# A graph kernel of four layers: how layer 0 turns its adjacency tiles and counts in-degrees

## The chip, the cores and the metric

The kernel runs on one core of a Trainium2 chip. A core has TensorE (PE: matrix products from SBUF into PSUM, with the stationary operand loaded by a separate instruction, PEld), VectorE (DVE), ScalarE (ACT), GpSimd (POOL), SyncE (SP, which here only issues DMAs) and 16 DMA engines. PSUM has eight banks that each hold 512 words of 4 bytes in each of 128 partitions. Every engine works through its own instructions in order; a DMA queue is filled by the engine that issues it.

The metric is the device time of one execution in microseconds (us), as the median of several. The change is judged against the kernel before on the same chip.

## The reference, cut to what matters

There are 2708 nodes with 512 features. `adj` is a symmetric 0/1 matrix of int32 with ones on its diagonal, but the kernel doesn't rely on the symmetry: layer 0 multiplies with the transposed matrix, layers 1 to 3 with the matrix itself.

```python
def _L0_gnn_ref(X, adj, weight):
    a = adj.astype(X.dtype)
    out = (a.T @ X) @ weight
    in_degree = a.sum(axis=0)
    norm = jnp.clip(in_degree, 1.0, None) ** (-0.5)
    return jax.nn.relu(out * norm[:, None])

def _L1_gnn_ref(X, A, W_nb, b_nb, W_line, b_line, neibor_num):   # 64
    Ab = A > 0
    keep = Ab & (jnp.cumsum(Ab.astype(jnp.int32), axis=1) <= neibor_num)
    cnt = keep.sum(axis=1, keepdims=True).astype(X.dtype)
    nb_mean = (keep.astype(X.dtype) @ X) / jnp.maximum(cnt, 1.0)
    xj = jax.nn.leaky_relu(nb_mean @ W_nb.T + b_nb)
    xi = jax.nn.leaky_relu(X @ W_line.T + b_line)
    return xi + jnp.where(cnt > 0, xj, 0)
...
# each layer: h = relu(layernorm(x)); x = x + layer(h, adj, ...)
```

Layer 2 is masked attention with eight heads, layer 3 a mean over neighbours. Layer 1 keeps the first 64 neighbours of a row, so it needs the column of the 64th one; layers 1 and 3 need the row's degree.

## The kernel before

**Tiling.** Nodes are cut into `NC` = 22 chunks of `R` = 126, the last one with 62. Layer 0 goes over `adj` once, in six groups of columns (`sizes` = 4, 4, 4, 4, 3, 3 chunks) and, within a group, over the 22 row chunks `m`. One step of this double loop is a unit; there are 132. For the chunks of a group, accumulators `acc` of one PSUM bank each stay open over the 22 units. The features enter as `h0[m]`, the product of the normalized x and the layer's weight, split by `halves` into two fp32r parts so that two fast products stand for one exact one. The last chunk has both parts in one tile, its second one in the rows from `TAIL` = 64, and needs one product.

**A unit's stages.** `staged` (L219) writes the loops out with a lag for each stage:

- lag 0, `load0` (L427): one DMA from SP brings 126 rows of `adj`, 506 columns wide, into `ai` (five buffers). In the first group the chunk of x is loaded, normalized, turned and multiplied by the weight beside it (`dense`, L229).
- lag 4, `count0` (L445): DVE casts `ai` to fp32r `ar` (L450), ACT squares it to bf16 `ab` (L452), DVE runs a cumulative sum along the columns into `cum` (L458) and stores its last column in `deg` (L466), from which the next group goes on.
- lag 5, `sign0` (L469): ACT's Sign of 63.5 - `cum`, with a sum over the columns, which tells where the 64th neighbour stands.
- lag 6, `multiply0` (L483): on PE eight products (four chunks, two halves; six in a group of three) with `ar` as the stationary operand (L348), then one product with `ab` for each chunk against an identity with ones beside it (`ident1`, L501). The latter turns the tile and sums its columns at once. DVE copies the sums out (L504), ACT copies the turned tile as int8 into `vT` (L513). With the last row chunk the column sums are added up (L508), the norm is made (L509 to L511), and after the products each accumulator is evacuated with relu and norm, by ACT and DVE in turn (L531, L535); POOL, or DVE in the last group, adds the old x (L537).
- lag 6, `save0` (L540): ACT's queue stores the x of the group before.

`vT` stays in SBUF, one tile for each group, and is read by layers 1 to 3: `vT[g][:, k, :]` has a column of `adj` in each partition and all rows along it.

**Buffers.** All PSUM tiles of this part share one ring of eight banks (`ps`, L123). `ar` and `ab` have three buffers each, `cum` two, x five (`XBUFS`); `hn` and `y` share a ring `t` of three.

**The hand-over to layer 1.** `stages1` is layer 1's `dense`: load x, normalize, turn, multiply by two weights (`product1`, L596). Its first three steps are put into the last group of layer 0 (`AHEAD`, at m = 9, 13 and 18); the others follow it. Beside them run `save_last` (lag 3), which stores the last group's x, and `spread_last` (lag 4), which spreads the columns of the 64th neighbours over all partitions (`lastr`). `rdeg` and `rcnt` are made from `deg` by DVE (L572 to L576). Then `aggregate` (L356) multiplies `h1` with `vT`, masked by `lastr` in `weight1` (L621).

**Order.** The program order of the loops is a priority. The scheduler of the language puts an instruction ahead of others on its engine when by its model it is ready earlier; on the chip each engine then keeps that order.

## Time and profile before

| What | us |
|---|---|
| median of three executions (lowest, highest) | 1851.69 (1848.1, 1854.51) |
| the profiled execution, its own time | 1852.72 |
| its span, first to last instruction | 1850.8 |
| first products of layer 0 (`acc`) start | 55.47 |
| last products of layer 0 (`acc<-tail`) start | 399.86 |
| layer 1's `nb_ps` and `line_ps` products, `acc`, on the chain of waits | from 413.58 |
| layer 1's aggregation, one piece of the chain | 570.63, for 188.72 |

The profile is one execution's record. A group of instructions has its line in the code, engine, operation, output and input tiles with their sizes, how many there were, busy us and the mean ns of one, then the idle time that the engine had just before them and what ended it. Durations of matmuls are modelled and overlap; the distance between starts tells PE's rate. Waits are put down to the semaphore that came last.

The same page shows how PE's products stand beside the loads of their stationary operand, and the share of DMA queues:

```profile
L348 PE MATMUL acc<-halves,ar 126*126 126x512 f32 x924 | 253.2, 413 | 6.5 <-ACT vT L513 3.5 <-DVE ar L450 2.6 <-DVE deg L466 0.3
L348 PEld LDWEIGHTS acc<-halves,ar 126*126 126x126 f32 x924 | 163.8, 187 | 51.0 <-issue 9.2
L473 ACT ACTIVATE cum<-cum,limit 126x504 int16<-126x504 int16 (+3 forms) x132 | 88.4, 670 | 62.1 <-DVE deg L466 60.0
...
q1 hardware_dynamic: 106812, 123.60, 23.1%
q10 hardware_dynamic: 18484, 33.28, 5.4%
```

q1 is the queue that SP fills, q10 that of ACT. Loads of `adj`, loads of x and the copies between layers are on q1.

### The profile page before, as it was taken

To read this page: it belongs to the slowest core of one execution; us is meant where nothing else is said; L and a number is where in the kernel's file an instruction comes from. 1 tells how busy PE (TensorE), PEld (TensorE's weight loads), DVE (VectorE), ACT (ScalarE), POOL (GpSimd) and SP (SyncE) were. 2 spreads that over 40 slices of the span, in tenths; PEclk is the share of its full clock that TensorE was granted. 3 is DMA by queue.
4 is the path that set the end of the run, shared out by engine and by line. 5 is a ranking of instruction groups with operands and counts; after the bars stand their busy time and mean duration, and the time that the engine had idled before them with its cause. 6 is when DMAs were issued, how large, how long until landed. Compare 5 with 4: busy or idle time off the path is not lost.

```text
span 1850.8 us, 30734 instructions
## 1 busy us (share of the span) xinstructions
PE 1805.7 (98%) x11878; PEld 1050.0 (57%) x11878; DVE 1323.8 (72%) x1997; ACT 843.7 (46%) x1536; POOL 211.8 (11%) x190
## 2 busy tenths in 40 slices
PE   9999999889999999999999999999999999999998
PEld 4556667654446887754444344444344455478786
DVE  4755888874444566687889999999999777533334
ACT  2545887762220000056697776776743566500000
POOL 0001011211110112156100000000000222100000
PEclk9999999999999999999999999999999999999999
DMA  7323555542223112253330220121112444303221
GB/s 243 117 79 106 150 161 149 144 127 65 68 73 82 45 45 67 65 159 102 96 91 18 60 56 15 56 61 40 29 32 51 119 137 133 103 23 105 96 67 44
DMA packets 126027, 161.03 MB, mean 87 GB/s; under 512 B 57394, under 2 KB 77982, under 8 KB 124990
## 3 DMA queue, kind: packets, MB, share of 16 engines
q1 hardware_dynamic: 106812, 123.60, 23.1%
q10 hardware_dynamic: 18484, 33.28, 5.4%
q0 software_dynamic: 576, 2.10, 0.3%
q8 instruction: 95, 1.56, 0.3%
q14 instruction: 60, 0.49, 0.1%
HBM read 111.34 MB, written 47.42 MB: 86 GB/s over the span
## 4 chain that ended last, share of the span: by engine, by line
PE 61%; DVE 16%; issue 5%; DMA 4%; ACT 2%; POOL 0%; SPq 0%; DVEq 0%; ACTq 0%; POOLq 0%
PE acc L348 25%; PE av L945 10%; DVE t L762 9%; PE nb_ps L186 8%; PE sums L945 4%; PE wh_ps L186 4%; PE self_ps L186 4%; PE line_ps L186 4%; DVE cum L458 4%; DMA rb<-rT 2%; PE hT_ps L214 1%; DMA ai<-in_adj 1%; DMA x<-x 1%; DVE ar L450 1%; ACT cum L473 1%
## 5 line engine op out<-in xcount | busy, mean ns | idle before, releaser
L762 DVE SCALAR_TENSOR_TENSOR t<-rb,ec,vT 126x2708 f32<-126x2708 f32 (+2 forms) x220 | 532.6, 2471 | 21.5 <-PE sums L945 12.4
L348 PE MATMUL acc<-halves,kt 126*126 126x512 f32 x1848 | 434.8, 395 | 3.7 <-DVE kt L623 2.1
L945 PE MATMUL av<-t,whs 126*32 126x451 f32 (+3 forms) x4576 | 436.6, 515 | 1.3 <-ACT whs L751 0.8
L348 PEld LDWEIGHTS acc<-halves,kt 126*126 126x126 f32 x1848 | 342.6, 186 | 92.5 <-DVE kt L623 6.2
L945 PEld LDWEIGHTS av<-t,whs 126*32 126x32 f32 (+1 forms) x4576 | 161.9, 110 | 205.5 <-issue 180.1
L348 PE MATMUL acc<-halves,ar 126*126 126x512 f32 x924 | 253.2, 413 | 6.5 <-ACT vT L513 3.5
L780 ACT ACTIVATE b<-t,eb 126x2708 bf16<-126x2708 f32 (+1 forms) x78 | 199.0, 2552 | 21.6 <-DVE t L762 21.4
L348 PEld LDWEIGHTS acc<-halves,ar 126*126 126x126 f32 x924 | 163.8, 187 | 51.0 <-issue 9.2
L623 DVE SCALAR_TENSOR_TENSOR kt<-lastr,index,vT 126x504 fp32r<-126x504 int16 (+3 forms) x154 | 110.4, 728 | 81.7 <-PE acc L348 81.5
L195 ACT ACTIVATE ln_rs<-ln_mv,eps 126x1 f32<-126x1 f32 x88 | 25.6, 294 | 283.9 <-DMA x<-x 199.2
L1170 DVE CAST kt<-vT 126x504 fp32r<-126x504 int8 (+3 forms) x154 | 56.0, 366 | 137.8 <-PE acc L348 137.8
L458 DVE TENSOR_TENSOR_SCAN cum<-ai,deg 126x504 int16<-126x504 int32 (+2 forms) x110 | 126.0, 1156 | 32.9 <-DMA ai<-in_adj 21.5
L945 PE MATMUL sums<-t,whs 126*32 126x338 f32 (+5 forms) x1568 | 141.0, 451 | 5.6 <-ACT out L984 5.6
L751 ACT ACTIVATE whs<-wh,ef 126x64 f32<-126x64 f32 x220 | 76.3, 349 | 128.3 <-PE sums L945 73.1
L912 POOL TENSOR_SCALAR z<-y 126x512 f32<-126x512 f32 x22 | 44.0, 2001 | 666.9 <-DVE y L905 658.2
L473 ACT ACTIVATE cum<-cum,limit 126x504 int16<-126x504 int16 (+3 forms) x132 | 88.4, 670 | 62.1 <-DVE deg L466 60.0
L945 PEld LDWEIGHTS sums<-t,whs 126*32 126x32 f32 (+1 forms) x1568 | 56.0, 109 | 73.3 <-issue 39.1
L191 DVE BATCH_NORM_STATS2 ln_st<-x 126x6 f32<-126x512 f32 x88 | 60.4, 686 | 48.7 <-DMA x<-x 40.9
L513 ACT CAST vT<-vT_ps 126x504 int8<-126x504 f32 (+1 forms) x132 | 70.1, 536 | 29.2 <-DVE sums L504 20.0
L186 PE MATMUL nb_ps<-wfn,hT 128*126 128x512 f32 x176 | 81.2, 605 | 2.0 <-ACT hT L216 2.0
L186 PE MATMUL nb_ps<-wn,hT 128*126 128x512 f32 x176 | 81.4, 606 | 0.0
L186 PE MATMUL h_ps<-w0s,hT 128*126 128x512 f32 x176 | 79.9, 597 | 1.4 <-ACT hT L216 1.1
(178 smaller groups left out, 1972.7 us busy)
## 6 DMA issues: line engine op xcount, KB each, us to landing
x<-x SPq DMA_DIRECT2D x105, 252.0 KB
x<-x ACTq DMA_DIRECT2D x84, 252.0 KB
ai<-in_adj SPq DMA_DIRECT2D x84, 249.0 KB
x<-in_x SPq DMA_DIRECT2D x42, 252.0 KB
rb<-rT SPq DMA_DIRECT2D x7, 1332.8 KB
wh<-whd SPq DMA_DIRECT2D x70, 94.5 KB
whd<-wh SPq DMA_DIRECT2D x21, 252.0 KB
aT<-avT SPq DMA_DIRECT2D x21, 252.0 KB
```

Source lines behind the costliest of these rows:

```text
L186: nc.tensor.matmul(po[:n], lhsT[:, f, :n], w[:, f, :], start=(f == 0), stop=(f == NF - 1))
L191: nc.vector.bn_stats(st[:n], xc[:n])
L348: nc.tensor.matmul(acc[:R], weight[:, k * R : (k + 1) * R], parts[:, i, :], start=(m == 0 and i == 0), stop=(m == NC - 1),)
L458: nc.vector.tensor_tensor_scan(cum[:n, :gw], ai[:n, :gw], ai[:n, :gw], 0.0 if g == 0 else deg[:n, m : m + 1], op0=ALU.add, op1=ALU.max,)
L473: nc.scalar.activation(cum[:n, :gw], cum[:n, :gw], AF.Sign, bias=limit[:n], scale=-1.0, accum_out=signs[:n, m, g : g + 1],)
L513: nc.scalar.copy(vT[g][:, :, m * R : (m + 1) * R], pt[:R, :K, :R])
L623: nc.vector.scalar_tensor_tensor(by_chunk(kt, cs), lastr[:, cs[0] * R : (cs[-1] + 1) * R].rearrange("p (c r) -> p c r", r=R), index[:R, m ...
L751: nc.scalar.activation(t[:q, :O], wh.pop((u, m))[:q], AF.Copy, scale=by)
L762: ins = nc.vector.scalar_tensor_tensor(t[:q, : hi - lo], row[h][:q, lo:hi], ec[:q, m, h : h + 1], vT[g][:q, k, lo:hi], op0=ALU.max, op1=AL ...
L780: nc.scalar.activation(b[:q, : hi - lo], weight[s][:q, : hi - lo], AF.Sigmoid, bias=eb[:q, m, h : h + 1], scale=STEEP,)
L945: nc.tensor.matmul(p[j * S : (j + 1) * S, : b - a], lhsT, rhs[:, part * size + a : part * size + b], start=(s % NC == 0), stop=(s % NC == ...
L1170: nc.vector.tensor_copy(by_chunk(kt, cs), pattern(m, cs))
```

## The change

Row chunks are taken in pairs. The 252 rows of chunks 2b and 2b+1 are dealt out so that the first holds the even rows and the second the odd ones (`paired`); the last 188 rows keep their natural order for the products. One DMA loads a pair: partition r of `ai` gets rows 2r and 2r+1 side by side. `ai` has three such double buffers in place of five single ones. For the last pair a second copy, in even and odd rows, is loaded beside the natural one (`both`).

- `ar` is now ACT's Square of `ai`, which also sums its row into `squares`. DVE's cast is gone, and so is `ab`; `squares` takes the place of `ind` in a later test of the input.
- DVE forms `two` = 256 x odd + even as int16, once a pair: two bytes that are the entries of two neighbouring rows. A DMA stores it in DRAM (`packed`), and a transposing DMA, one for each chunk of columns (`turn0`), reads 1360 rows x 128 columns of int16 back, so that partition = column and the bytes along it = rows in natural order. That is `vT`, now uint8 with 128 partitions. The turns of a group are issued in the next group at m = 4, 7, 10 and 13, those of the last group in layer 1's steps (`turn_last`, lag 4). PE's turns, DVE's copies of the sums and ACT's copies into `vT` are gone.
- The in-degrees come from products of ones (32 columns) with the upper 16 bits of `ar`, for both chunks of a pair in one block, chunk k into partitions 32k to 32k+31 of one bank (`sums_ps`) that stays open over the group. At m = 20 it is copied out, turned (`by_row`) and made into the norm, one unit before the group's end.
- Chunk 19's old x is loaded into the ring `t` in place of the ring of x.
- `deg` is in paired order: it goes through DRAM (`degd`) to come back in natural order as `rdeg`, from which `rcnt` is made. `spread_last` puts `lastr` into natural order and moves from lag 4 to lag 8.

```diff
+    oneb = const.tile([P, 32], BF16, name="oneb")
+    nc.gpsimd.memset(oneb, 1.0)
...
+    def paired(src, c):
+        if c >= NC - 2:
+            return natural(src, c)
+        first = c // 2 * 2 * R
+        return src[first : first + 2 * R, :].rearrange("(r e) d -> e r d", e=2)[c % 2]
...
             def load0(i):
...
-                ai = wk.tile([R, WG + P - R], I32, name="ai", bufs=5)
+                ai = wk.tile([R, 2, WG + P - R], I32, name="ai", bufs=3)
+                q = min(2 * R, N - m * R) // 2
+                block = adj[m * R : m * R + 2 * q, c0 : c0 + wide]
+                pairs = block.rearrange("(r e) w -> r e w", e=2)
+                if m < NC - 2:
+                    nc.sync.dma_start(ai[:, :, :wide], pairs)
+                    both = ai
+                else:
+                    both = wk.tile([R, 2, WG + P - R], I32, name="ai", bufs=3)
+                    nc.gpsimd.memset(both[:, :, :wide], 0)
+                    nc.sync.dma_start(both[:q, :, :wide], pairs)
+                    nc.gpsimd.memset(ai[:, 1, :gw], 0)
+                    nc.sync.dma_start(ai[:, 0, :gw], block[:R, :gw])
+                    move(nc.sync, ai[:last_rows, 1, :gw], block[R:, :gw])
+                    move(nc.sync, ai[TAIL : TAIL + last_rows, 1, :gw], block[R:, :gw])
...
             def count0(i):
...
-                nc.vector.tensor_copy(ar[:, :gw], ai[:, :gw])
-                nc.scalar.activation(ab[:n, :wide], ai[:n, :wide], AF.Square)
+                nc.scalar.activation(
+                    ar[:, :gw], ai[:, :gw], AF.Square, accum_out=squares[:R, m, g : g + 1]
+                )
...
+                if both is not None:
+                    two = wk.tile([R, WG + P - R], I16, name="two", bufs=1)
+                    nc.vector.scalar_tensor_tensor(
+                        two[:, :wide], both[:, 1, :wide], 256.0, both[:, 0, :wide],
+                        op0=ALU.mult, op1=ALU.add,
+                    )
...
             def sign0(i):
...
+                if two is not None:
+                    q = min(R, PAIRS - m // 2 * R)
+                    to = packed[g][m // 2 * R : m // 2 * R + q, :]
+                    nc.sync.dma_start(to, two[:q, : to.shape[1]])
+
+            def turn0(g, k):
+                nc.sync.dma_start(
+                    vT[g][:, k, : 2 * PAIRS].bitcast(I16),
+                    packed[g][:, k * R : k * R + P],
+                    transpose=True,
+                )
+                nc.gpsimd.memset(vT[g][:, k, N:], 1)
 
             def multiply0(i):
...
-                for k in range(K):
-                    nc.tensor.matmul(
-                        pt[:, k, :], ab[:n, k * R : k * R + P], ident1[:n], start=True, stop=True
-                    )
-                nc.vector.tensor_copy(sums[g][:, :K, m : m + 1], pt[:R, :K, R : R + 1])
...
-                nc.scalar.copy(vT[g][:, :, m * R : (m + 1) * R], pt[:R, :K, :R])
+                for j in (i, i + 1) if m % 2 == 0 else ():
+                    q = rows(m + j - i)
+                    for k in range(K):
+                        nc.tensor.matmul(
+                            sums[g][k * 32 : (k + 1) * 32],
+                            oneb[:q],
+                            tiles[j].bitcast(BF16)[:q, 2 * k * R + 1 : 2 * (k + 1) * R : 2],
+                            start=(j == i and m == 0),
+                            stop=(j > i and m == NC - 2),
+                        )
...
+                if g and m in (4, 7, 10, 13) and m // 3 - 1 < len(groups[g - 1]):
+                    turn0(g - 1, m // 3 - 1)
...
+        nc.sync.dma_start(
+            degd[:even].rearrange("(b f) r -> b (f r)", f=2).rearrange("b (r e) -> r b e", e=2),
+            deg[:R, :even].rearrange("r (b e) -> r b e", e=2),
+        )
+        nc.sync.dma_start(degd[even:].rearrange("c r -> r c"), deg[:R, even:])
         rdeg = const.tile([P, NC], F32, name="rdeg")
+        nc.gpsimd.memset(rdeg, 1.0)
+        nc.sync.dma_start(rdeg[:R], degd.rearrange("c r -> r c"))
```

## The prediction, made before the change was run

> **What bounds the kernel now.** First the page's busy times: TensorE (PE) is busy for nearly the whole span, and the change touches only layer 0 and its hand-over to layer 1.
>
> ```profile
> PE 1805.7 (98%) x11878; PEld 1050.0 (57%) x11878; DVE 1323.8 (72%) x1997; ACT 843.7 (46%) x1536; POOL 211.8 (11%) x190
> L458 DVE TENSOR_TENSOR_SCAN cum<-ai,deg 126x504 int16<-126x504 int32 (+2 forms) x110 | 126.0, 1156 | 32.9 <-DMA ai<-in_adj 21.5
> ```
>
> Second, busy time in the five groups after the first (their ends are the `acc<-tail` matmuls of the PE timeline: 173.72, 222.60, 272.55, 321.75, 363.01, 399.86 us). Columns: stretch, busy us of each engine, clock, DMA share, GB/s. PE leads, but DVE (85%) and ACT (81%) are close and DMA is half used.
>
> ```profile
> 174.00:222.00 48.00, 46.38 (x256) 34.04 (x255) 39.63 (x89) 37.07 (x85) 7.19 (x6) 1.00 0.52 151
> 222.00:272.00 50.00, 47.70 (x258) 34.31 (x259) 42.68 (x95) 40.37 (x93) 7.19 (x6) 1.00 0.53 155
> 272.00:321.00 49.00, 47.34 (x261) 34.26 (x259) 42.41 (x94) 40.33 (x93) 7.18 (x6) 1.00 0.52 153
> 321.00:363.00 42.00, 37.27 (x206) 26.12 (x204) 34.49 (x95) 31.91 (x88) 6.94 (x8) 1.00 0.51 147
> 363.00:400.00 37.00, 36.43 (x202) 26.07 (x201) 32.51 (x125) 31.17 (x95) 8.25 (x25) 1.00 0.40 117
> ```
>
> Third, the operations that the change takes away or moves, by shape, from 174 to 400 us:
>
> ```profile
> L501 PE MATMUL vT_ps<-ident,ab 126*128 126x128 bf16 x378 | 39.3, 222 | 2.3 <-ACT y L535 1.9 <-ACT vT L513 0.3
> L513 ACT CAST vT<-vT_ps 126x504 int8<-126x504 f32 x68 | 38.4, 571 | 12.7 <-DVE deg L466 8.6 <-DVE sums L504 3.8
> L450 DVE CAST ar<-ai 126x504 fp32r<-126x504 int32 x65 | 31.6, 487 | 5.2 <-PE acc L348 5.2
> L504 DVE COPY sums<-vT_ps 126x4 f32<-126x4 f32 x68 | 10.3, 157 | 0.0
> ```
>
> Fourth, PE's timeline inside a group (start, duration): eight products, four turns, again. A unit takes 282.58 - 280.43 = 2.15 us. Layer 1 runs the same products without turns (chain of waits: 188.72 us for 814, 0.232 us each), so eight cost 1.86 and the four turns 0.29 us, although their own starts spread over only 0.21.
>
> ```profile
> 280.43 2.10 PE L348 MATMUL acc<-halves,ar 126*126 126x512 f32 x8
> 282.37 0.40 PE L501 MATMUL vT_ps<-ident,ab 126*128 126x128 bf16 x4
> 282.58 2.10 PE L348 MATMUL acc<-halves,ar 126*126 126x512 f32 x8
> ```
>
> Fifth, where PE stands still: at group boundaries (here the third group begins), and where layer 1 begins. The brackets hold the idle time and what ended it.
>
> ```profile
> 226.08 0.73 PE L348 MATMUL acc<-halves,ar 126*126 126x512 f32 x2 [0.96 <-ACT vT L513]
> 227.07 1.42 PE L348 MATMUL acc<-halves,ar 126*126 126x512 f32 x5 [0.26 <-ACT vT L513]
> 229.09 0.38 PE L501 MATMUL vT_ps<-ident,ab 126*128 126x128 bf16 x4 [0.60 <-ACT y L535]
> ```
>
> ```profile
> 412.50 1.07 PE L214 MATMUL hT_ps<-ident,hn 126*128 126x126 f32 x4 [4.38 <-DVE hn L205]
> ```
>
> The brackets at the five boundaries add to 7.9 us (0.9, 2.8, 1.7, 1.4, 1.1); inside the groups PE waits three times for DVE `ar`, 2.6 us (1.94 of it at 343.37). By its units alone a group of four would take 20 x 2.15 + 3.37 = 46.4 us and one of three 20 x 1.63 + 2.6 = 35.2; the five are 16.5 us longer than that, of which the brackets name 10.5. So the turns and these stalls are on the path; the casts and copies of ACT and DVE matter only through the stalls.
>
> **What the skill says.** "TensorEngine Tiling (Array Packing)", Key Properties: 32-column tiles run in parallel, and changing the tiling mode drains the engine. Layer 2 agrees with the first: eight 32-column bf16 products of 338 columns start within 0.29 us (1340.24 to 1340.53). A change of width costs little: a one-column product starts 0.33 us after a 512-column one (usually 0.232), and the next wide one 0.1 after.
>
> ```profile
> 1340.24 0.51 PE L945 MATMUL sums<-b,parts 126*32 126x338 bf16 x8
> 1340.53 2.50 PE L945 MATMUL av<-t,whs 126*32 126x451 f32 x24
> ```
>
> "DMA: Bandwidth & Descriptors", the section on why a DMA increments its semaphore by 16: the number of engines is the largest k up to 16 that divides the outer dimensions. The trace agrees: while the last 46 output rows are stored (1846.65 to 1848.05), the queue uses 2 of 16 engines.
>
> ```profile
> q1 hardware_dynamic: 31, 0.06, 11.8%
> ```
>
> The same page, "Latency and other measured facts", gives 261 GB/s for transposing DMAs; no transposing DMA is in this trace.
>
> **The change, part by part.**
>
> PE, inside groups. A pair of units now pays 2 x 0.29 = 0.58 us for turns (four chunks), 2 x 0.24 = 0.47 (three chunks: 327.71 - 326.09 = 1.62 us a unit less six products). In its place comes one block of sums a pair: 8 or 6 products of 126 columns into 32-column strips. Bounds: 0.1 us if they pack as tightly as layer 2's, 0.9 us if each pays the turn's 0.07 and each switch 0.15. I take 0.24 for the products (the 36 ns spacing of layer 2, less for fewer columns, more for the two-byte stride), 0.18 for two switches, and 0.08 for the first wide weight load, which today also follows the turns: 0.50 and 0.45. That gains 0.08 x 44 pairs in the groups of four (11 of the 44 in the first group) and 0.02 x 22 in the groups of three: 4 us. So swapping PE work for PE work gives almost nothing.
>
> ACT loses `vT` (0.57 us a unit) and gains an accumulator read (0.19); `Square` stays and now writes `ar`. DVE loses `ar` and `sums` (2 x 0.64 = 1.29 us a pair) and gains `two`; the nearest row, L623, is 0.73 us for the same operation and width. Both engines get about 0.5 us a pair of slack. On the path this removes the stalls inside groups. One wait is new: `two` has a single buffer, so DVE's next `two` waits for the packed store of the pair before; behind it stand the scan, `deg` and the norm, for which ACT's signs and the evacuations wait. A store has a pair's time, 4.2 us, and loads of twice its size land in 2.7 to 2.8 us when nothing is ahead of them (chain, 203.43 and 207.91): taken at nothing, 1 us a pair (66 us) if that cover is gone for good, which only a DMA queue that is always full would do.
>
> Boundaries. Today the norm waits for the last unit's turns, their copies and a reduction, and new turns need banks that old accumulators hold. Afterwards the norm is ready a unit earlier. What is late next: the block of sums comes first in a group and needs a ninth bank, so it waits for the first accumulator's evacuation, 0.68 us of ACT, of which three last products (0.7) cover part. I take 1.0 us a boundary for banks and small stalls (bounds 0 and today's 3.3), and data apart (below).
>
> DMA. A group of four carries 7.5 MB today (153 GB/s x 49 us). Added: 11 packed stores of 127 KB, four transposes of 1360 x 256 B = 348 KB (an estimate of 1.3 us each from the skill's 261 GB/s) and a second copy of the last pair, 0.38 MB: 10.7 MB, share 0.52 to about 0.75. Mean rate suffices; bursts hurt. On SP the store, waiting for DVE, stands before the next pair's load; a transpose waits for all stores of its group, the last of them four units old; POOL's fill of its last columns waits for it in turn, and behind that only residual adds of the group's end. The second copy of the last pair has 94 rows, so k = 2: 188 runs of 2024 B at the 2-engine rate seen at the end (31 packets of 2 KB in 1.4 us, 45 ns each) take 8.5 us, and the next pair's load queues behind it on two engines. Three pair buffers give a load about four units, 8.6 us, before the squares need it. So it is about hidden; bounds 0 and 6 us a boundary, I take 0.9.
>
> Entry to layer 1. One residual moves to another ring, so the third x load no longer waits for a save (4.3 us) and its own 3.4 us. 4.4 us of stall go; the degrees' round trip through DRAM on SP, 2520 and 2772 single words, and the last group's three transposes stand before the next loads. Bounds: gain 4.4, loss 8. PE has two to three chunks of 6.9 us to hide it; I take a gain of 3. The spreads of `last`, four steps later, lie beside PE's products.
>
> Sum. A group of four: 10 pairs x (16 x 0.232 + 0.50) = 42.1, last pair 12 x 0.232 + 0.50 = 3.3, boundary 1.0: 46.4. A group of three: 10 x (12 x 0.232 + 0.45) + 2.5 + 1.0 = 35.8. Three and two: 210.8, and 0.5 for layer 1's early turns: 211.3, where today 173.72 to 399.86 is 226.1: -14.8, 3 from the swap and 12 from stalls. First group -0.9, entry -3, two-engine loads 5 x 0.9 = +4.5. Together -14. The profiled execution took 1852.7 us (span 1850.8), 1.0 above the median of three: 1838.7, say 1839.
>
> **Rivals.**
> - Forecast, 1830 to 1846: 0.42.
> - PE reaches its product rate: sums pack to 0.1 us and no boundary stalls: -0.4 x 66 pairs, -4.5, -5: about 1812 to 1830. For it: layer 1's 188.72 us without a stall. Against: a switch costs something. 0.12.
> - No change, 1846 to 1857: the block of sums costs 0.7 us, which is +13 and cancels the boundaries. For it: the drain; against: the 0.1 us seen around narrow products. 0.15.
> - Slower: the last pair's second copy. If SP issues it before the pair's own rows, or the next pair comes two units late, squares and PE wait 6 us at each of five boundaries: +30 - 14, about 1868. It decides once landing takes more than the four units of lead. For it: k = 2, and DMA waits of 2.5 to 4.4 us already in the chain. Against: PE has rarely waited for data. With packed stores late behind loads (one buffer for `two`) adding to it: 0.31.
>
> Under 0.3% (5.5 us) a measurement of this kernel can't be told from no change. Faster 0.54, same 0.15, slower 0.31. The likeliest case's own range is 1830 to 1846; with the others, 1818 to 1868.
>
> **What would show it.** The five groups take about 46 and 36 us; the block of sums takes about 0.5 us between products; no stall ends with DVE `ar`; the stall before layer 1's third turn is gone. Wrong if PE waits for ACT squares or DMA at each group's start, if DVE stands before `two`, or if transposes take over 5 us.

## The result and the profile after

| | before | after |
|---|---|---|
| median of four executions (lowest, highest), us | 1851.71 (1848.1, 1854.51) | 1921.05 (1916.96, 1928.38) |
| span of the profiled execution, us | 1850.8 | 1915.0 |
| first products of layer 0 start, us | 55.5 | 54.5 |
| first group, us | 118.2 | 123.2 |
| the five other groups, us | 48.9, 50.0, 49.2, 41.3, 36.9; together 226.1 | 61.2, 62.3, 64.5, 49.7, 54.1; together 291.8 |
| end of layer 0 to layer 1's aggregation, us | 170.5 | 168.9 |
| from there to the end, us | 1280.4 | 1276.5 |

The ratio after to before is 1.038, 95% interval 1.0343 to 1.0416: slower by 69 us where 13 us of gain were forecast. The parts of the table add up to the 64.2 us between the spans: -1.0 + 5.0 + 65.7 - 1.6 - 3.9. The five groups hold the loss. (A group is counted from one start of `acc<-tail` to the next; the sums are rounded once, the expectations below have 226.2 and 291.9.)

The page's busy times, and the two groups of instructions that stand for the waits, of the changed kernel:

```profile
PE 1823.6 (95%) x11884; PEld 1064.8 (56%) x11884; DVE 1304.2 (68%) x1792; ACT 803.4 (42%) x1542; POOL 217.7 (11%) x203
...
L494 DVE TENSOR_TENSOR_SCAN cum<-ai,deg 126x504 int16<-126x504 int32 (+2 forms) x110 | 128.4, 1178 | 49.9 <-DMA ai<-in_adj 44.0
L522 ACT ACTIVATE cum<-cum,limit 126x504 int16<-126x504 int16 (+3 forms) x132 | 88.2, 668 | 119.7 <-DVE deg L502 113.5
```

ACT and DVE did get lighter (ACT 843.7 to 803.4, DVE 1323.8 to 1304.2 us), as the change means them to. But DVE's scan now stands 44 us before loads of `adj` where it stood 21.5, and ACT's Sign waits 113.5 us for that scan where it waited 60.0. PE's share fell from 98% to 95% although its busy time rose by 18 us. The busy times by group say how both can be (columns as before: stretch, busy us of PE, PEld, DVE, ACT, POOL, granted clock, DMA share, GB/s):

```profile
178.00:239.00 61.00, 49.64 (x262) 35.39 (x261) 36.91 (x55) 30.74 (x87) 8.75 (x6) 0.92 0.55 159
239.00:301.00 62.00, 52.07 (x261) 37.05 (x260) 36.21 (x58) 32.34 (x93) 8.00 (x10) 0.86 0.64 165
301.00:366.00 65.00, 51.47 (x263) 36.95 (x264) 39.80 (x60) 33.49 (x97) 8.54 (x10) 0.89 0.66 165
366.00:415.00 49.00, 38.92 (x194) 26.66 (x192) 29.78 (x58) 25.52 (x85) 8.18 (x10) 0.92 0.63 163
415.00:470.00 55.00, 42.88 (x205) 28.99 (x205) 33.51 (x90) 28.03 (x98) 7.81 (x19) 0.87 0.57 137
sum 292.00, PE 234.99 PEld 165.04 DVE 176.21 ACT 150.12 POOL 41.28; mean PE 47.00 PEld 33.01 DVE 35.24 ACT 30.02 POOL 8.26
```

The same stretch of the kernel before in one row:

```profile
174.00:400.00 226.00, 215.12 (x1176) 154.79 (x1176) 191.72 (x493) 180.84 (x450) 36.75 (x51) 1.00 0.50 146
```

PE's idle time went from 226 - 215 = 11 us to 292 - 235 = 57 us: 46 us of the loss are PE standing still. The other 20 us are PE's work at a lower clock, 0.86 to 0.92 where it was 1.00. That it is the clock, and not the new block of sums, is seen in a run told of below, no_pack: with the same products at a clock of 0.99, PE is busy 213.9 us over its five groups (columns as above).

```profile
198.25:439.01 240.76, 213.87 (x1183) 152.54 (x1181) 141.78 (x266) 146.93 (x454) 29.90 (x25) 0.99 0.47 139
```

No engine and no mean DMA share is near its end (DMA 0.55 to 0.66); the loss is waiting, not work.

PE's timeline in the second group shows the good part and the bad part side by side (start, duration):

```profile
242.53 3.71 PE L369 MATMUL acc<-halves,ar 126*126 126x512 f32 x14
246.17 0.30 PE L558 MATMUL sums_ps<-ar,oneb 126*32 126x126 bf16 x8
246.40 3.98 PE L369 MATMUL acc<-halves,ar 126*126 126x512 f32 x16
250.31 0.30 PE L558 MATMUL sums_ps<-ar,oneb 126*32 126x126 bf16 x8
...
258.80 0.24 PE L558 MATMUL sums_ps<-ar,oneb 126*32 126x126 bf16 x4
264.10 0.30 PE L558 MATMUL sums_ps<-ar,oneb 126*32 126x126 bf16 x4 [5.06 <-ACT ar L488]
264.32 5.91 PE L369 MATMUL acc<-halves,ar 126*126 126x512 f32 x13
```

Where data are there, the block of eight sums costs 246.40 - 246.17 = 0.23 us, and a pair takes 250.31 - 246.17 = 4.14 us where two units before took 4.30. Then PE stands 5.06 us before the odd chunk's `ar`, and the products after that stall take 5.91 / 13 = 0.45 us each where 3.98 / 16 = 0.25 is usual. "TensorE: Matmul & The Clock Gate", section on HAM oscillation (HAM is its name for what sets TensorE's clock by how busy it is), says that idle gaps of over some 3.4 us let the clock be throttled; this stall agrees, and it makes each long stall cost more than its own length.

What the waits of the changed kernel between 178 and 470 us are (engine, line, what it waited for: us, times, longest):

```profile
ACT cum L522 <- DVE deg L502: 80.4, 54, 8.2
...
PE sums_ps L558 <- ACT ar L488: 52.4, 27, 5.1
DVE two L506 <- DMA packed<-two: 50.0, 15, 10.1
DVE cum L494 <- DMA ai<-in_adj: 35.2, 20, 7.4
ACT ar L488 <- DMA ai<-in_adj: 20.1, 10, 6.1
```

The profile puts the third of these lines down to the single buffer of `two`; the fourth and fifth are the loads. They hold DVE; DVE's scan holds ACT's Sign; behind that Sign stands the next square, and for the square PE waits.

The chain of waits around the start of the second group (start, us, what) has the longest of the loads:

```profile
214.67 1.27 DVE cum L494
215.94 0.58 DVE two L506
...
216.97 11.53 DMA ai<-in_adj
...
228.58 0.70 DVE two L506
229.29 5.25 DMA ai<-in_adj
...
234.63 2.43 DVE cum L494 x2
```

The 11.53 us are the second copy of the last pair, 94 rows; `two` can't be formed before it, DVE holds everything behind `two`, and the next pair's load ends 5.25 us after it. The timelines of SyncE's queue, of DVE and of ACT (start, duration) show how little lead the copy had and who stood behind it:

```profile
216.97 0.69 SPq L475 DMA_DIRECT2D ai<-in_adj  x1
...
217.79 0.15 DVE L502 CAST deg<-cum 126x1 f32<-126x1 int16 x1
228.58 0.69 DVE L506 SCALAR_TENSOR_TENSOR two<-ai 126x506 int16<-126x506 int32 x1 [10.64 <-DMA ai<-in_adj]
...
230.78 0.71 ACT L522 ACTIVATE cum<-cum,limit 126x504 int16<-126x504 int16 x1 [8.17 <-DVE deg L502]
231.49 0.61 ACT L488 ACTIVATE ar<-ai 126x504 fp32r<-126x504 int32 x1
```

The copy was issued at 216.97, behind a store for which the queue had waited for DVE; at 217.94 DVE had nothing left to do before it, and stood 10.64 us. While the copy's rest arrived alone, from 224.2 to 228.4 us, SyncE's queue used 13.1% of the 16 DMA engines, which is two:

```profile
q1 hardware_dynamic: 104, 0.21, 13.1%
```

The same happens where the next two groups end. The copies are issued at 280.36 and 344.53, and DVE forms their `two` 11.5 us later each time. Here the profile names another transfer, the store of the `two` before, which landed about then; that DVE waited for the copy as well is seen in the run two_t below:

```profile
291.83 0.69 DVE L506 SCALAR_TENSOR_TENSOR two<-ai 126x506 int16<-126x506 int32 x1 [10.14 <-DMA packed<-two]
356.08 0.69 DVE L506 SCALAR_TENSOR_TENSOR two<-ai 126x506 int16<-126x506 int32 x1 [10.07 <-DMA packed<-two]
```

The hand-over to layer 1, on PE's timeline:

```profile
478.74 0.59 PE L215 MATMUL hT_ps<-ident,hn 126*128 126x126 f32 x4
...
489.08 1.07 PE L215 MATMUL hT_ps<-ident,hn 126*128 126x126 f32 x4 [2.88 <-DVE ln_mv L194]
```

The third chunk's turn, at 478.74, has no bracket any more (4.38 us before), but a chunk later PE stands 2.88 us.

### The profile page after: what moved, and what is told of

It is laid out like the page before. It is cut to its first block, busy times and chain, and to the rows that moved or that the text cites. A ratio compares the mean times of both kernels' runs of the same rounds, so it can differ in the third digit from the quotient of the medians.

```text
span 1915.0 us, 30559 instructions
## 1 busy us (share of the span) xinstructions
PE 1823.6 (95%) x11884; PEld 1064.8 (56%) x11884; DVE 1304.2 (68%) x1792; ACT 803.4 (42%) x1542; POOL 217.7 (11%) x203
## 4 chain that ended last, share of the span: by engine, by line
PE 67%; DVE 13%; DMA 12%; issue 6%; ACT 2%; POOL 0%; SPq 0%; DVEq 0%; ACTq 0%; POOLq 0%
PE acc L369 25%; PE av L1038 12%; PE nb_ps L187 8%; DVE t L855 7%; DMA ai<-in_adj 6%; PE sums L1038 5%; PE wh_ps L187 4%; PE self_ps L187 4%; PE line_ps L187 4%; DVE cum L494 3%; DMA packed<-two 3%; PE hT_ps L215 2%; PE h_ps L187 1%; PE fused_ps L312 1%; DMA rb<-rT 1%
## 5 line engine op out<-in xcount | busy, mean ns | idle before, releaser
L855 DVE SCALAR_TENSOR_TENSOR t<-rb,ec,vT 126x2708 f32<-126x2708 f32 (+2 forms) x220 | 532.2, 2469 | 17.2 <-PE sums L1038 9.4
L1038 PEld LDWEIGHTS av<-t,whs 126*32 126x32 f32 (+1 forms) x4576 | 166.4, 110 | 199.3 <-issue 173.4
L369 PE MATMUL acc<-halves,ar 126*126 126x512 f32 x924 | 259.2, 431 | 1.0 <-ACT y L611 1.0
L369 PEld LDWEIGHTS acc<-halves,ar 126*126 126x126 f32 x924 | 179.5, 201 | 52.8 <-issue 6.1
L1263 DVE CAST kt<-vT 126x504 fp32r<-126x504 uint8 (+3 forms) x154 | 56.0, 365 | 138.2 <-PE acc L369 138.2
L522 ACT ACTIVATE cum<-cum,limit 126x504 int16<-126x504 int16 (+3 forms) x132 | 88.2, 668 | 119.7 <-DVE deg L502 113.5
L488 ACT ACTIVATE ar<-ai 126x504 fp32r<-126x504 int32 (+2 forms) x132 | 75.4, 572 | 61.8 <-DMA ai<-in_adj 25.7
L506 DVE SCALAR_TENSOR_TENSOR two<-ai 126x506 int16<-126x506 int32 (+2 forms) x66 | 44.3, 672 | 72.5 <-DMA packed<-two 53.6
## 6 DMA issues: line engine op xcount, KB each, us to landing
x<-x SPq DMA_DIRECT2D x105, 252.0 KB
x<-x ACTq DMA_DIRECT2D x84, 252.0 KB
x<-in_x SPq DMA_DIRECT2D x42, 252.0 KB
whd<-wh SPq DMA_DIRECT2D x21, 252.0 KB
aT<-avT SPq DMA_DIRECT2D x21, 252.0 KB
```

Source lines behind the costliest of these rows:

```text
L369: nc.tensor.matmul(acc[:R], weight[:, k * R : (k + 1) * R], parts[:, i, :], start=(m == 0 and i == 0), stop=(m == NC - 1),)
L488: nc.scalar.activation(ar[:, :gw], ai[:, :gw], AF.Square, accum_out=squares[:R, m, g : g + 1])
L522: nc.scalar.activation(cum[:n, :gw], cum[:n, :gw], AF.Sign, bias=limit[:n], scale=-1.0, accum_out=signs[:n, m, g : g + 1],)
L855: ins = nc.vector.scalar_tensor_tensor(t[:q, : hi - lo], row[h][:q, lo:hi], ec[:q, m, h : h + 1], vT[g][:q, k, lo:hi], op0=ALU.max, op1=AL ...
L1038: nc.tensor.matmul(p[j * S : (j + 1) * S, : b - a], lhsT, rhs[:, part * size + a : part * size + b], start=(s % NC == 0), stop=(s % NC == ...
L1263: nc.vector.tensor_copy(by_chunk(kt, cs), pattern(m, cs))
```

## The experiments

Eighteen kernels were run. Each was compared with the kernel before on the same chip. Where an edit leaves work out, the groups' lengths are what is read: the later layers then work on other bits.

| kernel | median, us | ratio to before (95%) | first group | five groups |
|---|---|---|---|---|
| before | 1851.7 | 1 | 118.2 | 226.1 |
| after | 1921.05 | 1.038 (1.0343 to 1.0416) | 123.2 | 291.8 |
| two_t | 1918.56 | 1.0374 (1.0338 to 1.0409) | 123.8 | 282.4 |
| store7 | 1920.01 | 1.0368 (1.0338 to 1.0399) | 124.1 | 286.7 |
| split | 1899.58 | 1.0271 (1.0225 to 1.0317) | 117.3 | 274.6 |
| one_copy | 1885.93 | 1.0185 (1.0155 to 1.0216) | 120.7 | 257.5 |
| no_turn | 1937.67 | 1.0477 (1.0447 to 1.0508) | 120.8 | 282.2 |
| no_store_both | 1892.34 | 1.0232 (1.0202 to 1.0262) | 114.5 | 244.6 |
| no_pack | 1886.78 | 1.0197 (1.0167 to 1.0226) | 114.1 | 240.8 |
| no_store_sign6 | 1890.16 | 1.0215 (1.0185 to 1.0244) | 112.7 | 250.7 |
| ar_dve | not read | | 126.5 | 271.7 |
| two_loads | 1879.61 | 1.0146 (1.0111 to 1.0182) | 114.1 | 260.1 |
| sign6 | 1877.61 | 1.0136 (1.0106 to 1.0165) | 119.3 | 245.4 |
| loads_sign6 | 1866.81 | 1.0077 (1.0048 to 1.0107) | 112.8 | 244.5 |
| loads_sign6_one | 1865.96 | 1.0079 (1.006 to 1.0098) | 112.7 | 252.0 |
| loads_store7 | 1863.17 | 1.0051 (1.0033 to 1.0068) | 112.7 | 244.9 |
| six | 1891.69 | 1.0225 (1.0201 to 1.0249) | 130.7 | 254.5 |
| six_one | 1901.61 | 1.0277 (1.0249 to 1.0305) | 131.8 | 267.0 |
| t2_before | 1856.79 | 1.0026 (1.0009 to 1.0043) | 117.5 | 233.4 |
| pair_t2_before | 1866.08 | 1.0083 (1.0054 to 1.0112) | 121.5 | 236.9 |

The lengths come from one profiled execution of each kernel; how far they vary from one execution to the next was not measured. Two kernels whose queues wait alike (two_t and store7) lie 4 us apart in the five groups, so a difference of 5 us or less is not leant on.

### The single buffer of `two`

two_t:

```diff
-two = wk.tile([R, WG + P - R], I16, name="two", bufs=1)
+two = common.tile([R, WG + P - R], I16, name="two", tag="t", bufs=3)
```

> The changed kernel with `two` moved from its single buffer into the ring `t` (three buffers, shared with hn and y). Theory A (DVE waits at `two` for the packed store of the pair before, and everything behind it on DVE is late): most of the 65 us go, about 1870 to 1885 us, and the waits of DVE `two` on the packed store, 53.6 us now, fall under 10. Theory B (the last pair's second copy on two DMA engines holds up the next group): less than 10 us, about 1912 to 1920. Theory C (stores and transposing DMAs make the queue late for the pair loads, of which only three are buffered): less than 15 us, since the loads stay as late; DVE then waits for `ai` instead.

Measured: 1918.56 us, no gain. The five groups, 282.4, are 9.5 us shorter in the profiled execution, but layer 0 began 5.4 us later in it. The waits of two_t between 184 and 467 us show why so little came:

```profile
DVE two L506 <- DMA ai<-in_adj: 58.9, 15, 11.4
PE sums_ps L558 <- ACT ar L488: 45.7, 28, 5.1
```

`two` no longer waits 50 us for its store but 58.9 us for a load (10.6 us in the changed kernel, in one wait). Four of these waits, 39.5 us together, are for the second copy; in the groups where the changed kernel's profile had named the store they are

```profile
297.16 0.69 DVE L506 SCALAR_TENSOR_TENSOR two<-ai 126x506 int16<-126x506 int32 x1 [10.97 <-DMA ai<-in_adj]
359.63 0.69 DVE L506 SCALAR_TENSOR_TENSOR two<-ai 126x506 int16<-126x506 int32 x1 [11.38 <-DMA ai<-in_adj]
```

So a large part of what the profile put down to the single buffer was the copy, and the buffer alone was worth nothing that can be measured in the whole time.

### The second copy of the last pair

split gives the 94 rows to two transfers, of 80 and of 14 rows:

```diff
-nc.sync.dma_start(both[:q, :, :wide], pairs)
+cut = q // 16 * 16
+nc.sync.dma_start(both[:cut, :, :wide], pairs[:cut])
+nc.sync.dma_start(both[cut:q, :, :wide], pairs[cut:])
```

> The changed kernel with the second copy of the last pair loaded as 80 + 14 rows in place of 94. Theory B: the load of 11.5 us falls to about 4, the groups' ends lose their wait and some 6 us in each of six groups go: about 1880 to 1890 us. Theory A: about 5 us or less, 1912 to 1920. Theory C: about 10 us.

one_copy takes it out altogether:

```diff
-both = wk.tile([R, 2, WG + P - R], I32, name="ai", bufs=3)
-nc.gpsimd.memset(both[:, :, :wide], 0)
-nc.sync.dma_start(both[:q, :, :wide], pairs)
...
+both = ai
...
```

> The changed kernel without the second copy of each group's last pair: the packed numbers of the last two chunks are formed from the rows as the products use them, so the last rows of vT are not the ones that layers 1 to 4 should see (every step after layer 0 does the same work on other bits). Everything else is as changed. If the second copy costs what `split` gave back and a little more (its pair buffer and its bytes go too): five groups 262 to 270 us in place of 291.9, total 1888 to 1898. If the second copy's cost is only the queue that it sits on: about as `split`, 272 to 276, total 1900. If the loop of three pair buffers is the whole loss: below 240, total 1868.

Measured: the five groups fall by 17.2 us with split and by 34.3 with one_copy; the medians by 21 and 35 us. So the copy with its pair buffer is half of what the groups lost, and half of that again is gained by sending its rows as 80 and 14. In split the copy at the first of these boundaries has landed 3.77 us after its second part is issued (chain of waits), and DVE stands 3.60 us for it where it stood 10.64; at the next two boundaries that `two` comes after both scans, and DVE does not stand before it:

```profile
212.81 3.77 DMA ai<-in_adj
...
216.71 0.69 DVE L508 SCALAR_TENSOR_TENSOR two<-ai 126x506 int16<-126x506 int32 x1 [3.60 <-DMA ai<-in_adj]
```

one_copy did better than its first expectation and well short of the last one: the copy is the largest single cause, not the only one.

### The transposes, the stores and the packing

no_turn leaves out the transposing DMAs, no_store_both also the stores and the second copy, no_pack also `two`:

```diff
-nc.sync.dma_start(vT[g][:, k, : 2 * PAIRS].bitcast(I16), packed[g][:, k * R : k * R + P], transpose=True)
-nc.gpsimd.memset(vT[g][:, k, N:], 1)
+nc.gpsimd.memset(vT[g][:, k], 1)
```

> The changed kernel without its transposing DMAs: vT is filled with ones, so layers 1 to 3 work on another pattern and only layer 0's time is to be read. Theory C: 20 us or more go in layer 0. Theories A and B: under 8 us. The range of single transposes: 22 times the estimate of 1.3 us is 29 us of queue time in all.

> The changed kernel without the packed stores, the transposing DMAs, `two` of the last pair and the second copy (vT filled with ones; only layer 0's time is to be read). What is left is the pair loads with three buffers, the squares on ACT and the sums from ones. If A, B and C are all there is, groups of four take 45 to 47 us and groups of three 35 to 37 as predicted, some 1835 to 1845 us in all; if they stay above 55, the pair loads themselves (theory D) are the cause.

> `no_store_both` without the packing on VectorE as well: no `two`, no stores, no transposes, no second copy (vT is filled with ones by GpSimd; every later step does the same work on other bits). What is left of the change in layer 0 is pair loads, the casts of ar by squares on ScalarE, and the sums by ones. If the packing holds the loop (VectorE's 0.7 us for a pair between two scans, which needs both halves): five groups 228 to 233 in place of 244.6. If the squares on ScalarE behind the Signs hold it: 240 to 245.

In all three the fills of `vT` were put at the start of the program, and layer 0 begins near 84 us in place of 54.5; their medians can't be compared, their groups can. Measured, five groups: 291.8 after, 282.2 without transposes (61.2, 62.3, 64.5 against 63.3, 61.4, 61.0 in the groups of four; the last group gains 7), 244.6 without stores and copy too, 240.8 without packing too. Read beside one_copy's 257.5, stores and transposes together cost 13 us once the copy is gone, the packing 4, which is within the spread. Even with nothing of the new path left but pair loads, squares and sums by ones, the groups take 14.6 us longer than before. PE is busy for 213.9 us of them (shown above), 215 before; it stands 26.9 us where it stood 11, and most of it for ACT's square, where the kernel before waited 2.6 us for DVE's cast:

```profile
PE sums_ps L540 <- ACT ar L486: 20.6, 26, 2.4
```

no_pack's waits of SyncE's queue (185 to 430 us) tell what the loads then stand before:

```profile
SPq L470 <- ACT ar L486: 90.3, 29, 5.4
SPq L470 <- ACT cum L510: 32.7, 11, 7.2
```

L470 is the load of a pair. Its buffer is free when the square of the odd chunk has read it, so a late square makes a late load, which makes a late scan and a late Sign, and the next square is behind that Sign. This ring is read from the waits; no run opens it cleanly.

### ScalarE's order, half loads, and the casts

sign6 (with split and two_t) issues the Sign one unit later, behind the next chunk's square, and gives `cum` a third buffer; two_loads (with split) brings each pair as two transfers; loads_sign6 has all of these; ar_dve (with split) gives the cast back to VectorE:

```diff
-cum = wk.tile([R, WG], I16, name="cum", bufs=2)
+cum = wk.tile([R, WG], I16, name="cum", bufs=3)
...
-(5, sign0),
+(5, store0),
+(6, sign0),
```

```diff
-nc.sync.dma_start(ai[:, :, :wide], pairs)
+for e in range(2):
+    nc.sync.dma_start(ai[:, e, :wide], pairs[:, e])
```

```diff
-nc.scalar.activation(ar[:, :gw], ai[:, :gw], AF.Square, accum_out=squares[:R, m, g : g + 1])
+nc.vector.tensor_copy(ar[:, :gw], ai[:, :gw])
```

> The split kept, `two` in the ring `t`, `cum` with three buffers in the space so won, and the Signs one unit later (lag 6; the stores stay at lag 5). Theory E: a square no longer waits behind the Sign of the unit before it, PE's waits on ACT `ar` (46.7 us with the split) fall to 15 or less: 1860 to 1875 us. Theory D: under 10 us, 1890 to 1900.

> The 80 + 14 split kept (1899.6 us), and each pair loaded by two DMAs, even rows first, into the same buffer. Theory D (pair loads: a buffer is filled and freed in pieces of 0.5 MB, so the loop load, scan, Sign, Square, next load is too long for three buffers): the first half lands some 2 us earlier, that is once a loop of two pairs, and the groups fall by 5 to 10 us each: 1860 to 1880 us. Theory E (the squares that PE needs stand on ACT behind Signs that wait for DVE's scan): under 10 us.

> The split kept, and `ar` cast by DVE as in the kernel before, ahead of the scan; ACT keeps the Signs alone, and the test that all entries are 0 or 1, which used the squares' sums, is left out. Theory E: PE's waits on `ar` fall and some 20 us go, although DVE gets 0.4 us a unit more: 1870 to 1885 us. Theory D: no gain, 1890 to 1905. If DVE becomes the bound, the units take 2.2 us and more and the time goes up.

> Both: the later Signs with three `cum`, `two` in the ring `t`, the split, and each pair in two loads. If D and E both hold, the gains add and the groups come to 48 and 38 us: about 1850 us. If one alone holds, this equals the better of the two single ones within 6 us. If neither, about 1895 us, and the queue's load (theory C) is what is left.

Measured, against split's 274.6 us in the five groups: sign6 245.4, two_loads 260.1, both 244.5, the cast on DVE 271.7. ar_dve makes the kernel take its general path after layer 0 (5989 us), so its whole time says nothing. Moving the cast gains nothing that can be told from the spread: DVE's busy time rises to 209 us of 272, and PE still waits 28 us for DVE's `ar` (47 for ACT's in split). sign6's edits and a load that is there by halves do help, but not one on top of the other: both together give no more in these groups than sign6 alone; in the first group half loads save 6.5 us (119.3 to 112.8). How much of sign6's 29 us is the order of ScalarE is not shown, since `two` in the ring of three and the third `cum` came with it and split with these two alone was not run.

no_store_sign6 tried the later Sign where stores, transposes and copy are left out:

> `no_store_both` (no stores, no transposes, no second copy; vT filled with ones) with `two` still made, in the ring of three, and the test of the row sums one unit later, behind the next chunk's square. If ScalarE's order holds the loop: five groups 228 to 234 in place of 244.6. If it is the packing: 241 to 246.

Measured 250.7 us, no better than no_store_both's 244.6: a miss. The same edits that help while stores and the copy are there don't help without them, so ScalarE's order is not shown to be a cause by itself. It is worth a look that sign6, with all of its stores, transposes and the split copy, has groups as short (245.4) as no_store_both, which has none: what remains against 226.1 is not the added traffic alone.

### What is left in the best variant

loads_sign6_one is loads_sign6 without the second copy; six gives it six buffers of one chunk for three of a pair; six_one is both.

```diff
-ai = wk.tile([R, 2, WG + P - R], I32, name="ai", bufs=3)
+ai = [wk.tile([R, WG + P - R], I32, name="ai", bufs=6) for e in range(2)]
```

> `loads_sign6` (`two` in the ring of three, the test of the row sums one unit later, half loads) without the second copy of the last pair, left out as in `one_copy`, and with the pair buffers as in the change. If the second copy's buffer and bytes at the boundary are what is left (five groups 244.5 against 226.2): 228 to 234, total 1850 to 1856, within 0.3% of the kernel before. If half loads, and the wait of each pair for its buffer, are what is left: 240 or more, total 1862 to 1867.

> `loads_sign6` with the three buffers of a pair made into six of one chunk, so that the even chunk's buffer can be filled again as soon as its own square, its own scan and the packing have read it. Nothing is left out. If what is left of the loss (five groups 244.5 against 226.2) is that a pair is held as one: 234 to 238, total 1857 to 1861. If the loads wait for bandwidth or for the queue rather than for a buffer: 242 to 246, total 1865 to 1869. If more and shorter loads delay the stores: over 248, over 1870.

> `six` without the second copy of the last pair (left out as in `one_copy`). If the boundary of a group is the rest of the loss, since two buffers and 0.38 MB go to the second copy there: five groups 226 to 232, total 1848 to 1854, level with the kernel before. If the turned stores and the order on ScalarE are the rest: 236 or more, over 1857.

loads_sign6_one: 1865.96 us against 1866.81, nothing; its groups were even 7.5 us longer, and the hand-over to layer 1 as much shorter. In one_copy leaving out the copy was worth 34 us in the groups; with the other repairs in place it is hidden. The costs overlap, and their sizes can't be added.

six and six_one got slower, by 25 and 36 us against loads_sign6 and loads_sign6_one. 18 and 19 us of that lie in the first group, beside the loads of x. With more buffers the scheduler set ScalarE's instructions in another order: in six, from 74 to 84 us, a Sign that waits 4.04 us for DVE stands ahead of the turned x (`hT`), for which PE then waits 1.39 us. That this order is the whole loss is not shown. So these two don't answer what they were built for; whether a buffer for each chunk helps stays untried in a clean form.

store7 and loads_store7 issue the store of `two` two units later. In the changed kernel SyncE's queue stood for VectorE at the stores (L533) between 178 and 470 us, with the next loads behind:

```profile
SPq L533 <- DVE deg L502: 42.2, 21, 3.9
SPq L533 <- DVE two L506: 30.7, 16, 3.5
```

```diff
+(7, store0),
```

> `two_t` (`two` in the ring of three) with the store of `two` issued two units later than the scan of its row, so that it does not stand at the head of SyncE's queue while VectorE still works on `two`; nothing else is changed and nothing is left out. In the changed kernel SyncE waited 57 us (178 to 400 us of the span) for VectorE at these stores, with the next loads behind them. If that is a cause of its own: five groups 255 to 265 in place of 282.4, total 1890 to 1901. If the loads are held by their buffers and only trade one wait for another: 278 to 285, total 1914 to 1921.

> `loads_sign6` with the store of `two` two units later in the same way; nothing is left out. If what is left (five groups 244.5 against 226.2) is the store at the head of the queue: 228 to 234, total 1850 to 1856. If it is the buffers of the pairs, which ScalarE's squares set free: 242 to 247, total 1864 to 1869.

Measured: 1920.01 us against two_t's 1918.56, and 1863.17 against loads_sign6's 1866.81 (intervals of the ratios overlap); five groups 286.7 and 244.9. store7 hardly did what it was built for. Against two_t, on which it is built, the queue's wait for VectorE at the stores went from 63 us only to 60 (184 to 467 and 180 to 467 us), and the loads' own wait at the queue, for buffers mostly, stayed near 80. loads_store7 did take some away, 51 us to 36 (168 to 412 us), and its groups are as long as those of loads_sign6 (244.5). What a queue without any such wait would give is not known.

Last, the pair loads alone, in the kernel before. They need room, which t2_before makes by giving the ring `t` two buffers:

```diff
-ai = wk.tile([R, WG + P - R], I32, name="ai", bufs=5)
+ai = wk.tile([R, 2, WG + P - R], I32, name="ai", bufs=3)
...
+nc.sync.dma_start(ai[:, :, :wide], block.rearrange("(e r) w -> r e w", e=2))
```

> The kernel before with two buffers in place of three in the ring that holds y and the normalized x, which makes the room that pair_t2_before needs; a control, nothing is left out. Groups of 49 to 51 us with K=4 and 41 and 37 at the end as in the kernel before, total 1852 to 1875 since the later layers use that ring too.

> t2_before with the change's loads alone: two chunks by one transfer into three buffers of a pair, in the natural order of rows, in place of five buffers of one chunk; the turns on TensorE, the casts and the order of ScalarE stay as before, and nothing is packed, stored or loaded twice. If three buffers of a pair are what the changed kernel's loop cannot do without (six chunks held, but freed by two): the five groups grow by 12 to 25 us against t2_before. If the pair buffers only hurt together with the stores, the packing and ScalarE's later squares: within 5 us of t2_before.

Measured: 236.9 us against the control's 233.4, and 4.0 us more in the first group; 9 us in the medians. The first theory wanted 12 to 25 in the five groups; 3.5 lie within the spread. Six chunks' room in three pieces is nearly enough in the kernel before. (The control's two buffers of `t` cost its own groups 7 us against 226.1.)

No variant beat the kernel before; the nearest, loads_store7, is 0.51% slower (0.33 to 0.68%).

## Why the prediction was wrong

**PE's swap: right, and better than priced.** The block of sums was put at 0.50 us a pair; it costs 0.23, and a pair of units takes 4.14 us where the sum had 16 x 0.232 + 0.50 = 4.21. Eleven such pairs would make a group of some 45 us. "TensorEngine Tiling (Array Packing)", Key Properties, speaks of a drain at each change of mode; here two changes and eight products fit into 0.23 us.

**Relief of ACT and DVE: right as work, wrong as time.** Both engines got lighter, as forecast (33 us each by the 0.5 us a pair; ACT lost 40 over the whole program, DVE 20; that ACT was busy for 81% of the five groups was a slip for 80), but the step "On the path this removes the stalls inside groups" failed. In the sum it gave 12 us; in its place PE's stalls grew by 46 us and the clock cost 20 more. What ACT and DVE save in busy time comes back many times over in waits: in the changed kernel PE waits for a square on ACT, ACT for a scan on DVE, and DVE for a load, where before PE waited 2.6 us in all for DVE's cast.

**The second copy: the right rival at the wrong weight.** The slower rival named it, with its place and its cause, at 6 us a boundary. "DMA: Bandwidth & Descriptors", the section on the increment by 16, gives two engines for 94 rows, and the trace agrees with 13.1% of the 16 while the copy's rest arrives alone; the load was put at 8.5 us, the trace has 11.53, and split, whose 80 rows have 16 engines by the same rule, gets back 17.2 us. Taken out, it is worth 34.3 us in five boundaries, 6.9 each, near the rival's 6. The forecast took 0.9: "Three pair buffers give a load about four units, 8.6 us, before the squares need it" was the step that failed here. With that lead, 11.53 us would have cost some 3 (an estimate, 11.53 - 8.6). The lead was counted from the number of buffers and up to the squares; but the copy takes a pair buffer of its own, it stood in SyncE's queue behind a store that waited for DVE, and DVE's `two` asked for it: 1.0 us after it was issued (216.97 to 217.94), not 8.6. The wait was 10.6 us there, and 10.1 at the two boundaries after it. The prediction knew that a store waiting for DVE stands in this queue, but named it for the next pair's load only, and set no price on it.

**What no rival had.** The copy explains half. The slower rival ended at 1868 us; the measured 1921 has a second half of 31 us in the five groups. The sum took the waits for `two` at nothing, with 66 us "if that cover is gone for good, which only a DMA queue that is always full would do". The cover did go, at a DMA share of 0.55 to 0.66: DVE stood 50 us before `two` by the profile. But two_t shows that this wait was not a cause of its own, and that some 20 of the 50 us (10.14 and 10.07) ended as the second copy came in, which the profile did not name. "Mean rate suffices; bursts hurt" held and was not followed up: no price was set for a load that is late by a few us when a square, a scan and a Sign hang on it in a ring. Of this half, stores and transposes took 13 us with the copy gone; the packing (about 4) and the pair loads alone in the kernel before (3.5) lie within the spread. The 14.6 us that no_pack still loses come with pair loads, squares on ScalarE as the source of `ar`, and sums by ones; the wait seen there is PE's 20.6 us for the squares. What makes the squares late stays open: no_store_sign6 and ar_dve, which each loosened one link, brought nothing clear. Since the costs overlap, these figures are no parts of a sum.

**Transposes: right that the groups beside them don't grow; their size is not settled.** The prediction's estimate was 1.3 us each, with 5 us as the mark of wrong. What the trace has is how long each stood in SyncE's queue, not how long it took to land: the shortest 1.3 us, the median one 2.2 and the longest 5.6, past that mark (view of the line, instructions' durations: smallest, median, largest in ns):

```profile
L538 SPq DMA_TRANSPOSE vT<-packed x15: 1307/2167/5575, 236.8 to 430.8; - x15
```

Without them the groups of four are as long as with them, and the last group is 7 us shorter.

**Entry to layer 1.** 3 us of gain were taken, 1.6 came: the third turn's stall went as said, and a stall of 2.88 us at the next chunk took most of it back. The first group, put at -0.9, lost 5.0; with split it takes 117.3 us, but with one_copy 120.7, so how much of it is the copy is not clear.

## What to carry to other kernels

Before taking a wait in a tight loop at nothing because of a mean rate, follow one buffer around: who fills it, every engine that must read it before it is free, and what else stands in front of those reads. Count a transfer's lead from when it can be issued, behind what stands before it in its queue, to the first engine that asks for it: here 1 us, where the count of buffers gave 8.6. Three buffers of a pair did nearly as well as five of one chunk in the kernel before (236.9 against 233.4 us). A transfer of 94 rows was better sent as 80 and 14, and one that an in-order engine waits for must be priced at that engine, not at the matmul far behind it. Taking away the largest wait of a profile may bring nothing (50 us here), and the profile may name the wrong one of two transfers that land together; only runs that take out one part at a time, and then again beside other repairs, tell causes from covers.

## What the runs showed of the hardware

- Eight bf16 products of 126 columns into 32-column strips, between wide fp32r products, cost 0.23 us in all, changes of tile form included.
- After PE stood for 5.06 us, products took 0.45 us in place of 0.25; over the five groups the granted clock was 0.86 to 0.92, and PE was busy 235 us, where no_pack had the same products at 0.99 in 213.9.
- A load of 94 rows took 11.53 us and used two of 16 DMA engines at its end (13.1%); cut into 80 and 14 rows it landed 3.77 us after its second part was issued, and the five groups were 17 us shorter.
- Transposing DMAs that write 128 columns of 1360 two-byte words each left the length of the groups of four beside them unchanged (63.3, 61.4, 61.0 us without, 61.2, 62.3, 64.5 with); the last group was 7 us shorter without.
